# A conditioned transformer block: the first two norms with tokens on partitions, and five constant products ahead of them

## The chip, the cores and the metric

The kernel runs on one core of a Trainium2 chip. The metric is the device time of one execution in microseconds (us); lower is better. The median of three runs is given for a kernel. Five engines work side by side, each with its own queue of instructions: TensorE (PE in the profile; PEld is its loading of weights), VectorE (DVE), ScalarE (ACT), GpSimd (POOL) and SyncE (SP), which here issues most of the DMAs.

## The reference

One transformer block whose two norms are scaled and shifted by a condition `t` of each sequence. There are 4 sequences of 1024 tokens, 512 channels, 16 heads, a hidden width of 2048; everything is float32.

```python
def _tc_rmsnorm(x, t, gw, gb, bw, bb):
    g = (t @ gw.T + gb)[:, None, :]
    b = (t @ bw.T + bb)[:, None, :]
    inv_rms = jax.lax.rsqrt(jnp.mean(x * x, axis=-1, keepdims=True) + EPS)
    return g * x * inv_rms + b

def _L0_cond_ref(x, t, Wq, Wk, Wv, Wo, g1w, g1b, b1w, b1b, g2w, g2b, b2w, b2b, gate_w, hid_w, out_w):
    x = x + _attention(_tc_rmsnorm(x, t, g1w, g1b, b1w, b1b), Wq, Wk, Wv, Wo)
    return x + _swiglu(_tc_rmsnorm(x, t, g2w, g2b, b2w, b2b), gate_w, hid_w, out_w)

x = x + _L0_cond_ref(x, cond_256, ...)
```

The change touches only the first norm (g1, b1) of the first sequence, that is of its two halves of 512 tokens.

## The kernel before

Tokens come in eight blocks of 512, two to a sequence. A block lies in SBUF with channels on the 128 partitions: a tile `y[b, half]` of 128 x 4 x 512, where `C` = 4 groups of 128 channels stand side by side and the 512 tokens are columns. A norm therefore needs a sum over partitions for each token.

Up to line 740 lies the opening, with the tokens of the first sequence; after it the main loop runs over steps `g`. A step has the scores of one piece of attention on PE, the softmax of earlier ones on ACT and DVE, weighted values, and one or two chains of other work: first the projections that are left of the present and the next sequence (from `queue`), later the feed-forward network. At the end a short loop does what is left of the feed-forward network.

The order of the work on PE, DVE, ACT and POOL is the order in which the program issues it: each of these engines does its instructions one after the other, and one that waits holds up what is behind it. DMAs on SP are placed by a scheduler, so an early load can stand before the writes of the opening; each waits for its data and for a free buffer.

Buffers are named by a tag, with a number of buffers to each. The PSUM banks of tag `w` (pool `ps`, two of them) are shared by the sums of the norms (`pm`), the modulation (`pmod`) and two of three projections; the function `bank` gives every third projection the bank `wb` instead. In SBUF the squares of the opening and the staging of projected keys, queries and values take turns in tag `h` (seven buffers), the inverse of the first norm sits in tag `rmax`, that of the second in `tot`.

What the opening does, in the order of the program, is this:

- Loads on SP: the first half's tokens in four pieces (`load_y(0, 0)`), the modulation's weights for the first norm (`load_modw(0)`), weights of the first keys and queries (`load_wkq(0)`), the second half's tokens, the value weights `wv`, the modulation's second part, and two more weights of keys and queries.
- `norm_sum(y[0, 0], "a0_0")`, lines 210 to 220: for each channel group a square on ACT (line 215), and a product of the square with `ones_mean`, a 128 x 128 tile of 1/512 (line 216), all four summed in one PSUM bank. As the weights are all alike, each of the 128 partitions gets the mean of the squares for all 512 tokens. ACT takes the root (line 218), DVE the reciprocal (line 219), both of 128 x 512.
- `modulation(0)`: eight products of 128 x 128 weights with the condition, four columns each (line 722), and an addition on DVE (line 723).
- `norm_rest(0, 0, y[0, 0], "a0_0")`: for each channel group a multiplication by the inverse on DVE (`norm_scale`, line 199) and the modulation's scale and shift on ACT (`norm_mod`, line 202).
- Two projections of the first half, keys and queries (`project_kq`), eight products of 512 columns in all; every product goes through the helper `mm` (line 112).
- `norm_sum` for the second half, then the copies of the two projections out of PSUM on ACT with their DMA writes (the `evict` functions, lines 261 and 262).
- `norm_rest` for the second half.
- Four projections of values for the first half (`project_v`, lines 278 and 279 for copy and write); `modulation(1)`, for the second norm of the block, follows the first of them. Its weights share a buffer tag with the first residual load (line 435).
- One projection of keys for the second half. Then the main loop begins with the first scores (line 316).

The constant tiles that the change uses are there from the start: `ident`, the 128 x 128 identity, and `ones_mean`, which DVE fills at line 70.

Of the kernel before, what the change touches and what calls it, by code (L numbers as in the profile page):

```python
# [10 lines left out]
F32 = mybir.dt.float32  # L11
BF16 = mybir.dt.bfloat16
AF = mybir.ActivationFunctionType
ALU = mybir.AluOpType
# [3 lines left out]
P = 128  # L18
NB = 512
# [5 lines left out]
def tile_cond_transformer_block(  # L25
# [13 lines left out]
    nc = tc.nc  # L39
    NBLK, _, C, _ = x.shape  # L40
    B = cond_t.shape[1]
    D = C * P
# [3 lines left out]
    KT = L // P  # L46
# [11 lines left out]
    sb = ctx.enter_context(tc.tile_pool(name="sb", bufs=1))  # L58
    ps_sc = ctx.enter_context(tc.tile_pool(name="ps_sc", bufs=1, space=PSUM))
    ps_av = ctx.enter_context(tc.tile_pool(name="ps_av", bufs=1, space=PSUM))  # L60
    ps = ctx.enter_context(tc.tile_pool(name="ps", bufs=2, space=PSUM))
# [3 lines left out]
    ident = const.tile([P, P], F32, tag="ident", name="ident")  # L65
# [3 lines left out]
    ones_mean = const.tile([P, P], F32, tag="ones_mean", name="ones_mean")  # L69
# [3 lines left out]
    eps = const.tile([P, 1], F32, tag="eps", name="eps")  # L73
# [35 lines left out]
    def mm(dst, w, moving, start: bool, stop: bool, seeded: bool = False):  # L109
        n = columns[0]  # L110
        for k in range(0, P, n):
            nc.tensor.matmul(  # L112
                dst[k : k + n, :], w[:, k : k + n], moving, start=start, stop=stop, skip_group_check=seeded
            )

    y, wkq, wv, wo, kq, v = {}, {}, {}, {}, {}, {}
    raw, rmax, shift, mT, av, acc, avs, oT = {}, {}, {}, {}, {}, {}, {}, {}
    x2, res, h, fw, ow = {}, {}, {}, {}, {}
    bank_a, bank_b, fifth = {}, {}, {}
    state = {}  # L120
# [3 lines left out]
    def bank(name: str):  # L124

        if spare_bank[0]:
            spare_bank[0] = False
            return ps_av.tile([P, NB], F32, tag="av", name=name)
        turn[0] += 1
        if "sums" not in state and turn[0] % 3 == 0:  # L130
            return ps_b.tile([P, NB], F32, tag="wb", name=name)
        return ps.tile([P, NB], F32, tag="w", name=name)
# [65 lines left out]
    def norm_scale(dst, tag: str, c: int):  # L198
        nc.vector.tensor_tensor(dst[:, c, :], dst[:, c, :], state[tag], ALU.mult)

    def norm_mod(which: int, b: int, dst, c: int):
        nc.scalar.activation(  # L202
            dst[:, c, :],
            dst[:, c, :],
            AF.Identity,
            bias=mod[:, (2 * which + 1) * C + c, b : b + 1],
            scale=mod[:, 2 * which * C + c, b : b + 1],
        )

    def norm_sum(dst, tag: str):  # L210

        pm = ps.tile([P, NB], F32, tag="w", name=f"pm{tag}")
        for c in range(C):
            sq = sb.tile([P, NB], F32, tag="h", name=f"sq{tag}_{c}", bufs=7)
            nc.scalar.activation(sq, dst[:, c, :], AF.Square)
            nc.tensor.matmul(pm, ones_mean, sq, start=(c == 0), stop=(c == C - 1))
        inv = sb.tile([P, NB], F32, tag="rmax" if tag == "a0_0" else "tot", name=f"inv{tag}", bufs=1)
        nc.scalar.activation(inv, pm, AF.Sqrt, bias=eps)
        nc.vector.reciprocal(inv, inv)
        state[tag] = inv  # L220

    def norm_rest(which: int, b: int, dst, tag: str):
        for c in range(C):
            norm_scale(dst, tag, c)
            norm_mod(which, b, dst, c)
# [17 lines left out]
    def staging(name: str):  # L243

        if "sums" in state:
            return sb.tile([P, NB], F32, tag="ow", name=name, bufs=4)
        return sb.tile([P, NB], F32, tag="h", name=name, bufs=7)


    def project_kq(b: int, hg: int, which: int, half: int):  # L250
        pp = bank(f"pkq{b}_{hg}_{which}_{half}")
        for c in range(C):
            mm(pp, wkq[hg][:, which, c, :], y[b, half][:, c, :], c == 0, c == C - 1)

        def evict():
            scale = SCALE if which else 1.0
            if (b, hg) == (0, 0) and (which, half) != (1, 1):
                for i in range(NB // HQ):
                    k = half * NB // HQ + i
                    t = queries_tile(0, i) if which else keys_tile(0, k)  # L260
                    nc.scalar.activation(t, pp[:, i * HQ : (i + 1) * HQ], AF.Copy, scale=scale)
                    nc.sync.dma_start(out=kq_s[b, hg][:, which, k * HQ : (k + 1) * HQ], in_=t)
                return
            t = staging(f"st{b}_{hg}_{which}_{half}")
            nc.scalar.activation(t, pp, AF.Copy, scale=scale)
            nc.sync.dma_start(out=kq_s[b, hg][:, which, half * NB : (half + 1) * NB], in_=t)

        return evict

    def project_v(b: int, kt: int):  # L270
        half, col = divmod(kt * P, NB)
        pp = bank(f"pv{b}_{kt}")
        for c in range(C):
            mm(pp, y[b, half][:, c, col : col + P], wv[0][:, c, :], c == 0, c == C - 1)

        def evict():
            t = staging(f"sv{b}_{kt}")
            nc.scalar.copy(t, pp)
            nc.sync.dma_start(out=v_s[b][:, :, kt, :], in_=t.rearrange("p (a c) -> p a c", a=C))

        return evict
# [347 lines left out]
    for b in range(1, B):  # L629
        for half in range(QB):  # L630
            s = math.ceil((len(queue) + 1) / PACE)
            s4 = s - 4 - (s - 6) % UN
            tag = f"a{b}_{half}"
# [14 lines left out]
    for n in range(NBLK):  # L648
# [7 lines left out]
        if n < NBLK - 1:  # L656
            tag = f"f{n}"
# [30 lines left out]
    def fetch():  # L688

        if loads:  # L690
            load, a = loads.popleft()
            load(*a)
# [11 lines left out]
    with tc.manual_schedule(  # L704
# [8 lines left out]
        load_modw(1)  # L713
        fetch()
        fetch()
        norm_sum(y[0, 0], "a0_0")

        def modulation(k: int):
            pm = ps.tile([P, 4 * C, B], F32, tag="w", name=f"pmod{k}")
            cols = slice(k * 2 * C, (k + 1) * 2 * C)  # L720
            for i in range(k * 2 * C, (k + 1) * 2 * C):
                nc.tensor.matmul(pm[:, i, :], modw[:, i * P : (i + 1) * P], condT, start=True, stop=True)
            nc.vector.tensor_tensor(
                mod[:, cols, :], pm[:, cols, :], modb[:, cols].unsqueeze(2).to_broadcast([P, 2 * C, B]), ALU.add
            )

        modulation(0)
        norm_rest(0, 0, y[0, 0], "a0_0")
        evicts = [project_kq(0, 0, which, 0) for which in range(2)]
        norm_sum(y[0, 1], "a0_1")  # L730
        for evict in evicts:
            evict()
        norm_rest(0, 0, y[0, 1], "a0_1")
        for kt in range(KT // 2):
            project_v(0, kt)()
            if kt == 0:
                modulation(1)
        project_kq(0, 0, 0, 1)()

# [34 lines left out]
        while g < END:  # L774
# [10 lines left out]
            p = (g - FS) // 2  # L785
# [139 lines left out]
        for c, tag in enumerate(("rmax", "shift", "tot", "oT0")):  # L925
            sq = sb.tile([P, NB], F32, tag=tag, name=f"sqf{n}_{c}", bufs=1)
# [3 lines left out]
        for p in range(p0, NP_):  # L930
# [25 lines left out]
            if p == p0:  # L956
                pm = ps.tile([P, NB], F32, tag="w", name=f"pmf{n}")
                for c in range(C):
                    nc.tensor.matmul(pm, ones_mean, squares[c], start=(c == 0), stop=(c == C - 1))
                inv = sb.tile([P, NB], F32, tag="tot", name=f"invf{n}", bufs=1)  # L960
# [51 lines left out]
```

## Time and profile before

| what | value |
|---|---|
| runs before, median of 3 | 2450.79 us (2449.7 to 2451.94) |
| profiled execution, device time | 2455.29 us |
| profiled execution, span of its instructions | 2453.4 us |
| mean granted TensorE clock in it | 0.994 |
| PE busy | 2385.5 us (97%) |
| DVE busy | 1940.7 us (79%) |
| ACT busy | 1413.2 us (58%) |
| reciprocal of the opening's norms, DVE line 219 | 2 of 3353 ns |
| scaling in the opening, DVE line 199 | 8 of 686 ns |
| modulating in the opening, ACT line 202 | 8 of 801 ns |
| squares of the opening, ACT line 215 | 8 of 621 ns |

The span runs from the first to the last instruction; the device time has about 2 us around it. A line of a timeline has the start, the duration of the group, the engine, the line of the program, the operation, what it writes and reads, the shape and the count; in brackets stands the idle time of the engine before the group and what ended it. A line of a list of waits has the sum of the waits, their number and the longest. An instruction of PE that multiplies float32 appears as two passes, so that four products are x8. "PEclk" is the clock that TensorE was granted as a share of the full one; a stage's line gives for each engine its busy time within the stage.

### The profile page before, as it was taken

Reading aid. Unit: us, or ns where it says so; the run is one execution under the profiler, and the core shown is the slowest. Engines: PE = TensorE matmul, PEld = TensorE weight load, DVE = VectorE, ACT = ScalarE, POOL = GpSimd, SP = SyncE. Lnnn points to the kernel's source line nnn. Section 1 sums busy time; section 2 is a strip of 40 time slices with the busy share of each in tenths; the row PEclk is TensorE's granted clock in tenths of the full one; section 3 lists DMA queues with packets and bytes.
Section 4 is the critical chain, followed back from the end, with each engine's and each line's share of the span. In section 5 each row is a group of like instructions: output and inputs, shape, how many; then the busy total and the mean of one; then the engine's idle time right before and its main releaser. Section 6 shows DMA issues by size and latency. Waiting matters only on the chain. (4 is left out here: it accounts for less than half of the span.)

```text
span 2453.4 us, 72677 instructions
## 1 busy us (share of the span) xinstructions
PE 2385.5 (97%) x32553; PEld 1135.9 (46%) x32553; DVE 1940.7 (79%) x2183; ACT 1413.2 (58%) x1495; POOL 172.4 (7%) x207
## 2 busy tenths in 40 slices
PE   8999999999999999999999999999999999999999
PEld 3333334344444544544454544454445445444444
DVE  2688888878799988998899979997999799843332
ACT  3677776765566656665566656665666566512110
POOL 0000000000000000000000000000000000000000
PEclk9999999999999999999999999999999999999999
DMA  6599999988788788889888888898788888853442
GB/s 216 166 304 259 256 258 240 231 202 219 198 205 210 188 226 209 208 207 229 204 200 213 225 197 209 204 230 207 198 207 203 224 200 204 198 165 117 140 131 70
DMA packets 185988, 501.79 MB, mean 205 GB/s; under 512 B 21319, under 2 KB 78663, under 8 KB 158286
## 3 DMA queue, kind: packets, MB, share of 16 engines
q0 software_dynamic: 28656, 208.68, 43.9%
q1 hardware_dynamic: 156734, 288.47, 35.4%
q8 instruction: 256, 4.19, 0.7%
q14 instruction: 54, 0.44, 0.1%
q10 hardware_dynamic: 288, 0.01, 0.0%
HBM read 246.44 MB, written 41.97 MB: 118 GB/s over the span
## 5 line engine op out<-in xcount | busy, mean ns | idle before, releaser
L369 DVE TENSOR_TENSOR raw<-raw,shift 128x2048 f32<-128x2048 f32 (+1 forms) x320 | 588.8, 1857 | 25.6 <-ACT shift L364 25.6
L323 ACT COPY raw<-sc 128x2048 f32<-128x2048 f32 x256 | 479.7, 1874 | 187.4 <-PE sc L316 130.8
L372 ACT ACTIVATE raw<-raw 128x2048 f32<-128x2048 f32 x256 | 490.8, 1917 | 157.1 <-DVE raw L369 154.8
L328 DVE TENSOR_TENSOR rmax<-rmax,raw 128x1024 f32<-128x1024 f32 x384 | 469.5, 1223 | 48.8 <-ACT raw L323 42.2
L112 PE MATMUL pc<-h,ow 128*32 128x512 f32 x4096 | 470.5, 596 | 5.2 <-DMA ow<-in_out_w 4.2
L382 PE MATMUL av<-raw,v 128*32 128x256 f32 x4096 | 271.9, 383 | 35.6 <-ACT raw L372 35.1
L396 POOL DMA_DIRECT2D raw<-raw x192 | 165.3, 861 | 1967.4 <-ACT raw L372 878.9
L316 PE MATMUL sc<-q,k 32*128 32x256 f32 x4096 | 293.3, 400 | 1.0 <-ACT raw L323 1.0
L112 PE MATMUL pa<-x,fa 128*32 128x256 f32 x4096 | 272.5, 384 | 4.1 <-DVE pa L530 4.1
L112 PE MATMUL pa<-sums,fw 128*32 128x256 f32 x4096 | 271.5, 383 | 0.0
L112 PEld LDWEIGHTS pc<-h,ow 128*32 128x32 f32 x4096 | 128.6, 110 | 250.7 <-issue 231.9
L316 PEld LDWEIGHTS sc<-q,k 32*128 32x128 f32 x4096 | 184.9, 184 | 117.4 <-issue 75.8
L112 PE MATMUL pkq<-y,wkq 128*32 128x512 f32 (+1 forms) x1664 | 232.5, 594 | 4.3 <-ACT y L202 4.1
L112 PEld LDWEIGHTS pa<-x,fa 128*32 128x32 f32 x4096 | 124.7, 110 | 119.7 <-DVE pa L530 21.4
L382 PEld LDWEIGHTS av<-raw,v 128*32 128x32 f32 x4096 | 110.4, 109 | 149.4 <-ACT raw L372 66.0
L112 PEld LDWEIGHTS pa<-sums,fw 128*32 128x32 f32 x4096 | 134.4, 111 | 90.0 <-issue 3.4
L583 DVE SCALAR_TENSOR_TENSOR res<-pc,res 128x512 f32<-128x512 f32 x128 | 88.2, 689 | 78.9 <-PE pc L112 76.2
L545 ACT COPY pb<-pa 128x256 f32<-128x256 f32 x128 | 46.1, 360 | 174.4 <-PE pa L112 173.3
L562 ACT ACTIVATE t<-pa 128x512 f32<-128x512 f32 x128 | 78.1, 610 | 109.9 <-PE pa L112 109.6
L112 PE MATMUL pb<-x,fw 128*32 128x256 f32 x2048 | 134.0, 379 | 1.2 <-ACT pb L545 1.2
L112 PE MATMUL pa<-x,fw 128*32 128x256 f32 x2048 | 134.0, 379 | 0.0
L552 DVE TENSOR_TENSOR pb<-pb,p 128x256 f32<-128x256 f32 x128 | 55.0, 430 | 99.8 <-PE pb L112 94.2
(108 smaller groups left out, 2243.7 us busy)
## 6 DMA issues: line engine op xcount, KB each, us to landing
raw<-raw POOLq DMA_DIRECT2D x192, 1024.0 KB, 9.3
fw<-sw SPq DMA_DIRECT2D x128, 512.0 KB, 7.8
fa<-in_gh_w SPq DMA_DIRECT2D x128, 384.0 KB, 6.8
ow<-in_out_w SPq DMA_DIRECT2D x128, 256.0 KB, 3.1
wkq<-in_kq_w SPq DMA_DIRECT2D x32, 512.0 KB, 6.2
v<-vs SPq DMA_DIRECT2D x128, 128.0 KB, 6.6
k<-kqs SPq DMA_DIRECT2D x124, 128.0 KB, 6.5
kqs<-st SPq DMA_DIRECT2D x61, 256.0 KB, 8.3
```

The lines of the kernel that those rows point to most:

```text
L112: nc.tensor.matmul(dst[k : k + n, :], w[:, k : k + n], moving, start=start, stop=stop, skip_group_check=seeded)
L316: nc.tensor.matmul(sc[:, i, k, :], keys[rows, k * P : (k + 1) * P], queries[rows, :], start=True, stop=True)
L323: nc.scalar.copy(raw[r].rearrange("p k h q -> p h k q"), state.pop(("sc", r)))
L328: nc.vector.tensor_tensor(rmax[j], rmax[j], raw[r][:, k, :, :], ALU.max)
L369: nc.vector.tensor_tensor(t, t, s.unsqueeze(1).to_broadcast(list(t.shape)), ALU.add)
L372: nc.scalar.activation(raw[r], raw[r], AF.Exp)
L382: nc.tensor.matmul(av[j][i * DH : (i + 1) * DH, :], v[m, u][:, k, i * DH : (i + 1) * DH], raw[r][:, k, i, :], start=(kt == 0), stop=(kt == ...
L396: nc.gpsimd.dma_start(out=acc[j].rearrange("p k h q -> p (k h q)"), in_=raw[r].rearrange("p k h q -> p (k h q)"), accum_op=ALU.add,)
L545: nc.scalar.copy(bank_b[p][:, RIGHT], bank_a[p][:, RIGHT])
L552: nc.vector.tensor_tensor(b[:, LEFT], b[:, RIGHT], fifth.pop(p), ALU.subtract)
L562: nc.scalar.activation(state["t", p], bank_a[p], AF.Tanh, scale=0.5)
L583: nc.vector.scalar_tensor_tensor(r, pp, 0.5, r, ALU.mult, ALU.add)
```

## The change

`norm_sum` is rewritten. The four squares are now added up on DVE (three additions of 128 x 512). Four products then take 128 tokens each as weights and one column of `ones_mean` as the moving operand, so that the mean of token `p` of group `t` lands on partition `p` in column `t` of a 128 x 4 PSUM tile. Root (ACT) and reciprocal (DVE) are of 128 x 4. One DVE instruction multiplies the identity by these columns and by 512 into `diagonal`, four 128 x 128 diagonal matrices side by side. `norm_sum` returns a function `spread_root`, which multiplies `ones_mean` with the diagonals (512 columns): each partition gets the inverse of all 512 tokens, in PSUM, where `norm_scale` now reads it.

The caller issues `spread_root` of the first half after `modulation(0)`. For the second half the first projection of values, with its copy and its write, is moved ahead of `spread_root` and `norm_rest`; `modulation(1)` now follows the second projection of values. Ahead of the first `norm_sum` stand five products of `ones_mean` with itself, repeated to 512 columns, into a PSUM tile that nothing reads.

```diff
     def norm_sum(dst, tag: str):
 
-        pm = ps.tile([P, NB], F32, tag="w", name=f"pm{tag}")
+
+        sq = [sb.tile([P, NB], F32, tag="h", name=f"sq{tag}_{c}", bufs=7) for c in range(C)]
         for c in range(C):
-            sq = sb.tile([P, NB], F32, tag="h", name=f"sq{tag}_{c}", bufs=7)
-            nc.scalar.activation(sq, dst[:, c, :], AF.Square)
-            nc.tensor.matmul(pm, ones_mean, sq, start=(c == 0), stop=(c == C - 1))
-        inv = sb.tile([P, NB], F32, tag="rmax" if tag == "a0_0" else "tot", name=f"inv{tag}", bufs=1)
-        nc.scalar.activation(inv, pm, AF.Sqrt, bias=eps)
-        nc.vector.reciprocal(inv, inv)
-        state[tag] = inv
+            nc.scalar.activation(sq[c], dst[:, c, :], AF.Square)
+            if c:
+                nc.vector.tensor_tensor(sq[0], sq[0], sq[c], ALU.add)
+        nt = NB // P
+        pm = ps.tile([P, nt], F32, tag="w", name=f"pm{tag}")
+        for t in range(nt):
+            nc.tensor.matmul(pm[:, t : t + 1], sq[0][:, t * P : (t + 1) * P], ones_mean[:, 0:1], start=True, stop=True)
+        few = sb.tile([P, nt], F32, tag="few", name=f"few{tag}", bufs=2)
+        nc.scalar.activation(few, pm, AF.Sqrt, bias=eps)
+        nc.vector.reciprocal(few, few)
+        diagonal = sb.tile([P, nt, P], F32, tag="t", name=f"diagonal{tag}", bufs=2)
+        nc.vector.scalar_tensor_tensor(
+            diagonal,
+            ident.unsqueeze(1).to_broadcast([P, nt, P]),
+            float(D),
+            few.unsqueeze(2).to_broadcast([P, nt, P]),
+            ALU.mult,
+            ALU.mult,
+        )
+
+        def spread_root():
+            inv = ps.tile([P, NB], F32, tag="w", name=f"inv{tag}")
+            nc.tensor.matmul(inv, ones_mean, diagonal.rearrange("p t q -> p (t q)"), start=True, stop=True)
+            state[tag] = inv
+
+        return spread_root
...
-        norm_sum(y[0, 0], "a0_0")
+
+        ahead = ps.tile([P, NB // P, P], F32, tag="w", name="ahead")
+        for _ in range(5):
+            nc.tensor.matmul(
+                ahead, ones_mean, ones_mean.unsqueeze(1).to_broadcast(list(ahead.shape)), start=True, stop=True
+            )
+        spread_root = norm_sum(y[0, 0], "a0_0")
...
         modulation(0)
+        spread_root()
         norm_rest(0, 0, y[0, 0], "a0_0")
         evicts = [project_kq(0, 0, which, 0) for which in range(2)]
-        norm_sum(y[0, 1], "a0_1")
+        spread_root = norm_sum(y[0, 1], "a0_1")
         for evict in evicts:
             evict()
+        project_v(0, 0)()
+        spread_root()
         norm_rest(0, 0, y[0, 1], "a0_1")
-        for kt in range(KT // 2):
+        for kt in range(1, KT // 2):
             project_v(0, kt)()
-            if kt == 0:
+            if kt == 1:
                 modulation(1)
         project_kq(0, 0, 0, 1)()
```

## The prediction

> **What bounds the kernel now.** The page comes first: TensorE (PE) is busy 97% of the span, VectorE (DVE) 79%, ScalarE (ACT) 58%. The list of waits says how little PE waits on anything: 35.1 us for the exponentials in 37 pieces, and a few single ones, among them these.
>
> ```profile
> PE pma L216 <- ACT sqa L215: 5.5, 1, 5.5
> PE pc L112 <- DMA ow<-in_out_w: 4.2, 1, 4.2
> PE pkq L112 <- ACT y L202: 4.1, 1, 4.1
> POOL raw L396 <- DMA raw<-raw: 502.7, 54, 13.7
> ```
>
> So PE sets the end, and what brings its work forward in the opening brings the end forward, unless a later wait takes it back. I therefore read the opening in the timeline, first PE (start, duration, in brackets the idle time before):
>
> ```profile
> 5.49 5.17 PE L216 MATMUL pma<-sqa,ones_mean 128*128 128x512 f32 x8 [5.49 <-ACT sqa L215]
> 10.51 1.84 PE L722 MATMUL pmod<-condT,modw 128*128 128x4 f32 x16
> 16.41 9.97 PE L112 MATMUL pkq<-y,wkq 128*128 128x512 f32 x16 [4.05 <-ACT y L202]
> 26.21 3.60 PE L216 MATMUL pma<-sqa,ones_mean 128*128 128x512 f32 x8
> 30.59 3.70 PE L112 MATMUL pv<-wv,y 128*128 128x512 f32 x8 [0.78 <-ACT inva L218]
> 34.12 1.84 PE L722 MATMUL pmod<-condT,modw 128*128 128x4 f32 x16
> 36.61 10.57 PE L112 MATMUL pv<-wv,y 128*128 128x512 f32 x24 [0.64 <-DVE mod L723]
> 47.01 3.60 PE L112 MATMUL pkq<-y,wkq 128*128 128x512 f32 x8
> 50.54 1.15 PE L316 MATMUL sc<-q,k 32*128 32x256 f32 x16
> ```
>
> Every f32 product is two passes: the x8 at 47.01 are four products, 0.43 us a pass. The x16 at 16.41 take 9.80 us until the next start where 16 x 0.43 is 6.88. The stages by granted clock (span of the stage, PE busy, PEld, DVE, ACT, POOL, then PEclk) say why:
>
> ```profile
> 5.03:8.44 3.41, 2.95 (x4) 1.40 (x5) 0.00 (x0) 3.06 (x5) 0.00 (x0) 1.00 1.04 372
> 11.86:15.27 3.41, 0.49 (x5) 0.40 (x4) 3.41 (x3) 0.00 (x0) 0.00 (x0) 1.00 1.02 424
> 15.27:18.69 3.42, 2.29 (x3) 1.17 (x4) 2.04 (x4) 3.15 (x5) 0.00 (x0) 0.51 1.05 424
> 18.69:22.10 3.41, 3.41 (x5) 1.35 (x4) 0.00 (x0) 1.85 (x4) 0.00 (x0) 0.50 0.99 395
> 790.10:793.51 3.41, 1.64 (x32) 0.59 (x26) 3.41 (x6) 3.27 (x3) 0.51 (x1) 1.00 0.94 244
> 2169.08:2172.49 3.41, 1.66 (x28) 0.56 (x20) 1.23 (x1) 0.41 (x2) 0.00 (x0) 1.00 0.90 339
> ```
>
> The clock changes on a grid of 3.41 us. After the stage from 11.86, busy 0.49, it is halved; a stage with 2.29 busy does not restore it, one with 3.41 does, as 2.95 did at 8.44 (the recorded 1.00 before 8.44 is only the lack of a record: passes there took 0.85). Four stages in the body with 1.64 busy were each followed by a half clock; the one with 1.66 was not. So the limit for staying fast lies near 48% busy. The other engines (ACT's and DVE's timelines):
>
> ```profile
> 10.71 0.69 ACT L218 ACTIVATE inva<-pma,eps 128x512 f32<-128x512 f32 x1 [1.74 <-PE pma L216]
> 11.43 3.35 DVE L219 RECIPROCAL inva<-inva 128x512 f32<-128x512 f32 x1 [9.06 <-ACT inva L218]
> 14.81 2.50 DVE L199 TENSOR_TENSOR y<-y,inva 128x512 f32<-128x512 f32 x4
> ```
>
> The 3.35 us reciprocal of a whole 128x512 tile stands between the sums and the first scaling.
>
> **First norm.** The last square ends at 7.67. New: a DVE add of 0.69 (the 128x512 add of L141) to 8.41, the two earlier ones hidden under the squares; then eight narrow passes. No row has one column moving; the nearest, the modulation, does 16 passes in 1.84, so 0.92, and at most 8 x 0.25 (their full duration) = 2.0. I take 0.92: from 8.47, with 0.19 for the first weights, to 9.58, visible at 9.7. Root 0.30 and reciprocal 0.17 (the 128x4 rows of L173 and L177), diagonal 0.69 (scalar_tensor_tensor of L583; at most 1.23, the 128x1024 row of L328, for its broadcast operands): ready at 11.0. Meanwhile PE does the modulation, 1.84, to 11.42, its weights having landed at 8.4 (2.60 + 5.8). The spreading product, 0.43 + 0.59, ends at 12.44, so DVE scales from 12.49 where it was 14.81. Reading that operand from PSUM costs nothing visible: L583 reads PSUM and takes 689 ns against 684. **Gain 2.32.** With the narrow passes at 2.0, about 1.1 of it is lost. The key and query weights must be there at 14.09 (12.49 plus the present 1.60 from first scaling to first projection): they were issued at 3.08, ahead of the second half's tokens, whose transfers issued near 6 landed 6.5 later, so by 12.6.
>
> **The five products ahead** start near 1.1, when the memset of the ones is done (0.84 + 0.17), and wait for no DMA. Ten passes: at 0.85 until a full grid stage has gone by (5.0 in this execution's grid), then 0.43: done at 7.4; over all positions of the grid 6.9 to 8.8, so under the squares and the add that end at 8.4. Without that cover they would cost what they end later than 8.47. What they buy is a fast clock at 14.09. It holds if the gap from 12.44 to 14.09, 1.65 us, leaves every stage at least 1.76 busy: above 1.66, by 0.1. Then sixteen passes take 6.88, not 9.80: **gain 2.92** against this execution. It stood badly on the grid, though. Cold stretches last from about 2.6 us (a stage must be nearly full) to 6.0, mean 4.3, and cost half of that; this one ran 5.7. In the mean I take **2.2**; bounds 0 and 3.0.
>
> [...]
>
> **Second norm**, from the end of the projections to the first scores: 50.54 - 26.21 = 24.33 now. New: narrow passes 0.92 (for 3.60); the wait for the bank 0.39 (0.78 less the root's 0.69 - 0.30); the value projection now moved ahead 3.53; spreading product 0.86; three more projections 10.40; modulation 1.85; keys 3.53: 21.48. The wait of 0.64 for the modulation's add goes, since the projection after it takes another bank. **Gain 2.85.** The second diagonal is ready about 1.3 us after the sums, under the 3.53 of the moved projection; without that cover its reciprocal, add and diagonal would stand on PE, some 1.2. Behind it DVE scales 2.5 us while PE does the next projection (3.47), so the modulation's bank is free in time. The moved projection also issues an ACT copy (0.58), which now goes ahead of the four modulating activations, and one 256 KB write on SP; these writes are read back for products at 94.42. The modulation moves one projection back; SP's residual load, which waited for it at 36.00, still comes earlier, by about 4. POOL has nothing here.
>
> **Sum.** 2.32 + 2.92 + 2.85 = 8.1 on the profiled execution: 2455.29 (span 2453.4 and 1.9 around it) becomes 2447.2. The runs shown lie 4.5 lower, at 2450.79; with the mean clock term, 7.4 off: **2443.4**.
>
> **Rivals.** (1) The narrow passes do not count as busy: then from 7.4 to 14.09 only the 1.02 of the spreading product does, some stage falls under 1.65 whatever the grid, and the clock is halved again. Mean cold stretch as before, so no clock gain; spreading product +0.43, modulation about +0.5: 1.4 + 2.85 = 4.3, **2446.5**. For: 0.49 of such passes did not save the stage from 11.86. Against: no stage shows them alone. (2) The constants do not warm the clock, so the change does not do what it says: ten slow passes end at 9.7, narrow ones at double time (0.23) plus the modulation reach about 15.2, the first projection 18.9, 2.5 late; the second norm's 2.85 is left: **2450.5**. Against: the same ones with squares did warm it by 8.44. (3) Slower: the first output-weight load, PE's 4.2 us wait at 592 with a half clock after it, shares the DMA with 1 MB accumulations. Seven us earlier, it can fall behind one more; POOL's longest wait for one is 13.7. From 7.4 more waiting it decides; at 13.7, **2457.1**. For: DMA is over 80% busy there. Against: loads and products shift together.
>
> **Chances.** Forecast 0.56; rival 1 0.28; rival 2 0.07; rival 3 0.09. The runs of this kernel tell about 0.2% (4.9 us, the line at 2445.9) from no change. Faster: 0.54 of the forecast and 0.13 of rival 1 (its grid positions spread over +-1.7), 0.67. Same: 0.02 + 0.14 + 0.06 + 0.02 = 0.24. Slower: 0.07 of rival 3 and 0.01 each of rivals 1 and 2: 0.09. Range: low end the full 8.1 and one half-clocked stage of the body (1.7) less, 2441; high end rival 1 plus one such stage, 2448.5, which also covers the narrow passes at 2.0.
>
> **What would show it.** First scaling near 12.5, first projection near 14.1 with passes of 0.43 and no half clock before 50 us; first scores near 42.5; first projected value 0.4 after the narrow sums. Passes of 0.85 at 14.1 mean rival 1; slow narrow passes, rival 2; a wait over 11 us at the first output weights, rival 3. A first projection later than 15.5 with a fast clock would make the first step wrong.

## The result, and the profile after

The changed kernel takes 2443.22 us (median of 22 runs, 2440.21 to 2451.12), the kernel before 2450.14 us in as many runs beside them (2444.69 to 2455.69). The ratio of the two is 0.9975, with a 95% interval of 0.9968 to 0.9982. The forecast was 2443.4, worked out from three runs of the kernel before with a median of 2450.79.

The profiled execution of the changed kernel is the longest of its 22: 2451.12 us, with a span of 2449.3 against 2453.4. So its end says little, and its opening is read instead. First PE's timeline of the changed kernel (start, duration, what ended the idle time):

```profile
1.06 7.60 PE L739 MATMUL ahead<-ones_mean 128*128 128x512 f32 x10 [1.06 <-DVE eps L74]
8.74 1.05 PE L221 MATMUL pma<-ones_mean,sqa 128*128 128x1 f32 x8
9.66 1.93 PE L748 MATMUL pmod<-condT,modw 128*128 128x4 f32 x16
11.45 1.10 PE L237 MATMUL inva<-diagonala,ones_mean 128*128 128x512 f32 x2
14.18 8.74 PE L112 MATMUL pkq<-y,wkq 128*128 128x512 f32 x16 [1.63 <-ACT y L202]
22.76 0.95 PE L221 MATMUL pma<-ones_mean,sqa 128*128 128x1 f32 x8
24.06 3.70 PE L112 MATMUL pv<-wv,y 128*128 128x512 f32 x8 [0.35 <-ACT fewa L223]
27.60 1.02 PE L237 MATMUL inva<-diagonala,ones_mean 128*128 128x512 f32 x2
...
44.21 1.15 PE L336 MATMUL sc<-q,k 32*128 32x256 f32 x16
```

The first projections start at 14.18, where it was 16.41; their sixteen passes take 8.58 us until the next start, where it was 9.80; from there to the first scores it is 21.45, where it was 24.33. The first scores come 6.33 us earlier. DVE's timeline of the same kernel shows the first norm's small pieces and the scaling that follows them:

```profile
10.13 0.18 DVE L224 RECIPROCAL fewa<-fewa 128x4 f32<-128x4 f32 x1 [1.38 <-ACT fewa L223]
10.22 0.38 DVE L87 CAST select<-pick 12x512 bf16<-12x512 f32 x1
10.54 0.67 DVE L226 SCALAR_TENSOR_TENSOR diagonala<-ident,fewa 128x512 f32<-128x512 f32 x1
11.62 0.19 DVE L749 TENSOR_TENSOR mod<-pmod,modb 128x32 f32<-128x32 f32 x1 [0.41 <-PE pmod L748]
12.59 2.48 DVE L199 TENSOR_TENSOR y<-y,inva 128x512 f32<-128x512 f32 x4 [0.77 <-PE inva L237]
```

The small pieces cost what the prediction took from the nearest rows. A cast left over from the setup (0.38) slips in between, without harm: the diagonal is there at 11.21, and PE comes from the modulation to the spreading product only at 11.45. The scaling starts 2.22 us earlier than before.

But sixteen passes in 8.58 us are not 0.43 each. The stages of the changed kernel by granted clock (span, then PE, PEld, DVE, ACT and POOL busy, then PEclk, DMA share and GB/s) show a half clock exactly where the prediction had none:

```profile
7.21:10.62 3.41, 3.32 (x21) 2.25 (x19) 1.93 (x6) 2.16 (x3) 0.00 (x0) 1.00 1.00 349
10.63:14.04 3.41, 1.92 (x11) 1.09 (x10) 2.22 (x5) 0.73 (x2) 0.00 (x0) 1.00 1.05 430
14.04:17.45 3.41, 3.27 (x4) 1.51 (x5) 1.17 (x3) 3.41 (x7) 0.00 (x0) 0.50 1.01 412
```

PE was busy for 1.92 us of the middle stage and the clock fell to 0.50 after it; in the body of the kernel before, the stage from 2169.08, with 1.66, had kept it. What differs is what PE was busy with: 0.8 us of that stage are narrow passes of the modulation (four columns), only 1.1 the spreading product. The experiments ask whether that is the cause.

### The profile page after: what moved, and what is told of

The parts are those of the page before. It is cut to its first block, busy times and chain, and to the rows that moved or that the text cites. A ratio compares the mean times of both kernels' runs of the same rounds, so it can differ in the third digit from the quotient of the medians.

```text
span 2449.3 us, 72718 instructions
## 1 busy us (share of the span) xinstructions
PE 2389.4 (98%) x32567; PEld 1137.2 (46%) x32567; DVE 1940.2 (79%) x2191; ACT 1412.1 (58%) x1495; POOL 172.4 (7%) x207
## 5 line engine op out<-in xcount | busy, mean ns | idle before, releaser
L112 PE MATMUL pb<-sums,fa 128*32 128x256 f32 x2048 | 133.9, 379 | 0.0
```

Of the source, the lines that this page charges most:

```text
L112: nc.tensor.matmul(dst[k : k + n, :], w[:, k : k + n], moving, start=start, stop=stop, skip_group_check=seeded)
```

## The experiments

Theory A: a pass that streams few columns counts for little in whatever grants the clock, so the five products' fast clock is lost again before the first projections. Theory B: narrow passes count like others, and the half clock has another cause (the 1.63 us gap ahead of the projections) or is rare. Where PE stood in the profiled execution of each kernel (starts and durations in us; the passes are counted until the next start on PE):

| kernel | first projection | its 16 passes | first scores |
|---|---|---|---|
| before | 16.41 | 9.80 | 50.54 |
| changed | 14.18 | 8.58 | 44.21 |
| changed, second and third execution | 14.45, 13.94 | 8.98, 8.36 | 44.88, 43.75 |
| narrow products ahead | 17.56 | 9.12 | 48.14 |
| no products ahead | 16.91 | 9.46 | 47.82 |
| kernel before with products ahead | 17.60 | 10.04 | 51.97 |
| widened, two executions | 13.90, 13.86 | 6.97, 6.97 | 42.43, 42.39 |
| widened, gap filled, two executions | 13.80, 13.99 | 6.97, 6.97 | 42.32, 42.51 |
| gap filled only | 15.09 | 7.10 | 43.64 |
| first norm only | 14.00 | 8.58 | 48.61 |
| no move of the values | 14.75 | 8.59 | 46.10 |

### Narrow products alone ahead

```diff
-        for _ in range(5):
-            nc.tensor.matmul(
-                ahead, ones_mean, ones_mean.unsqueeze(1).to_broadcast(list(ahead.shape)), start=True, stop=True
-            )
+        for _ in range(18):
+            nc.tensor.matmul(ahead[:, 0, 0:4], ones_mean, ones_mean[:, 0:4], start=True, stop=True)
```

> The changed kernel with eighteen products of four columns (36 narrow passes) in place of the five of 512 columns. PE is then occupied from about 1.1 us on by narrow passes alone. Theory A (narrow passes do not count as busy): no full clock is granted before the first projections at 14 us are well under way; the narrow passes themselves, at a slow clock throughout, step by more than the 0.115 us of the modulation, about 0.2, and end near 8.7; passes of the first projections start at 0.85. Theory B (they count): the record shows a rise to the full clock between 4.5 and 8 us.

PE's timeline of this kernel, and three of its stages:

```profile
1.06 7.84 PE L739 MATMUL ahead<-ones_mean 128*128 128x4 f32 x36 [1.06 <-DVE eps L74]
8.76 1.85 PE L221 MATMUL pma<-ones_mean,sqa 128*128 128x1 f32 x8
10.47 3.55 PE L746 MATMUL pmod<-condT,modw 128*128 128x4 f32 x16
13.88 2.06 PE L237 MATMUL inva<-diagonala,ones_mean 128*128 128x512 f32 x2
17.56 9.29 PE L112 MATMUL pkq<-y,wkq 128*128 128x512 f32 x16 [1.62 <-ACT y L202]
```

```profile
4.86:8.27 3.41, 3.41 (x17) 3.41 (x18) 2.01 (x4) 2.53 (x4) 0.00 (x0) 1.00 1.01 362
18.52:21.93 3.41, 3.41 (x5) 1.35 (x4) 1.13 (x2) 3.18 (x6) 0.00 (x0) 1.00 0.56 234
21.94:25.35 3.41, 3.41 (x9) 1.52 (x8) 0.93 (x2) 0.00 (x0) 0.00 (x0) 1.00 0.00 0
```

The stage from 4.86 is filled by PE and by its weight loads, and the clock does not rise, although the record says 1.00 in it and in the others. The passes themselves tell: five 512-column passes in the full stage up to 21.93, nine in the next, so the rise came at 21.93; 0.213 us each in the modulation, (13.88 - 10.47) / 16, against 0.112 in the changed kernel, and 2.06 for the spreading product against 1.10. From 1.06 to 13.88 PE showed no idle time and stayed slow. So four-column passes did not raise the clock here, as theory A has it; whether they fail to keep it is the next question. There is one run of this kernel, 2449.93 us, too few to compare times.

### The narrow products widened

The four products of the sums and the eight of the modulation stream 128 columns; each overwrites what the one before left beyond its own columns.

```diff
-            nc.tensor.matmul(pm[:, t : t + 1], sq[0][:, t * P : (t + 1) * P], ones_mean[:, 0:1], start=True, stop=True)
+            nc.tensor.matmul(pm[:, t : t + P], sq[0][:, t * P : (t + 1) * P], ones_mean, start=True, stop=True)
...
-                nc.tensor.matmul(pm[:, i, :], modw[:, i * P : (i + 1) * P], condT, start=True, stop=True)
+                nc.tensor.matmul(
+                    wide[:, i * B : i * B + P].rearrange("p (r b) -> p r b", b=B),
+                    modw[:, i * P : (i + 1) * P],
+                    condT.unsqueeze(1).to_broadcast([P, P // B, B]),
+                    start=True,
+                    stop=True,
+                )
```

> The changed kernel with the narrow products widened: the four products of the sums and the eight of the modulation stream 128 columns each (the columns that are not needed are overwritten by the next product or not read), so that a pass is occupied by its columns for about 0.107 of its 0.115 us. Theory A (narrow passes do not count, which is why the clock fell at 14 us in the profiled execution of the changed kernel): no half clock between 8 and 40 us, sixteen passes of the first projections in 6.9 us, first scores at 42.5 to 42.8 us, and 1.3 to 3.0 us less than the changed kernel in the time. Theory B (it fell for another reason, such as the 1.63 us gap before the first projections): a half clock at 14 us again in about as many executions, and the same time as the changed kernel.

The 0.107 us there is an estimate, a quarter of the 0.43 us that a pass of 512 columns took in the kernel before.

PE's timeline of the widened kernel, and its stage before the projections:

```profile
9.46 1.95 PE L749 MATMUL pmod<-condT,modw 128*128 128x128 f32 x16
11.25 1.02 PE L237 MATMUL inva<-diagonala,ones_mean 128*128 128x512 f32 x2
13.90 7.13 PE L112 MATMUL pkq<-y,wkq 128*128 128x512 f32 x16 [1.63 <-ACT y L202]
20.87 1.05 PE L221 MATMUL pma<-ones_mean,sqa 128*128 128x128 f32 x8
```

```profile
10.66:14.08 3.42, 1.79 (x10) 0.96 (x10) 2.16 (x5) 1.05 (x2) 0.00 (x0) 1.00 1.07 437
14.08:17.49 3.41, 3.41 (x9) 1.49 (x10) 1.17 (x3) 3.41 (x7) 0.00 (x0) 1.00 0.99 402
```

The grid lies as in the changed kernel's profile (a stage ends at 14.08, there at 14.04), the gap of 1.63 us is the same, PE is even a little less busy (1.79 against 1.92), and the clock stays (1.00; the sixteen passes take 6.97 us). The wider passes cost nothing (1.95 us for sixteen against 1.93). The first scores come 1.78 us earlier than in the changed kernel. The median is 2442.84 us (9 runs), with a ratio to before of 0.9965 (0.9953 to 0.9977). These runs do not show the expected 1.3 to 3.0 us below the changed kernel; the runs of all kernels are put together further down.

### Without the five products, and the five products alone

The first takes the five products out of the changed kernel, the second puts them into the kernel before, ahead of its `norm_sum`.

> The changed kernel without the five products ahead. Theory A (the fast clock that they bring is lost again before the first projections): the sums and the modulation run at the slow clock, which puts the first projections 1 to 2.5 us later; their own slow stretch is as long on average as with the five products; time 1 to 2.5 us above the changed kernel. Theory B (in most executions the clock lasts until the projections): 2.2 us more on top of that, 3 to 5 us above the changed kernel.

> The kernel before with the five products ahead, nothing else. Both theories: the sums of the first norm run at the full clock, but they wait for the last square at 7.7 anyway and end about 1 to 1.5 us earlier at most (four products, 8 passes at 0.43, the last two after the last square); then 4 us of nothing on PE, so the clock is halved before the first projections as before. Time 0 to 2 us below the kernel before. If the five products were worth their 2.2 us by themselves, the first projections would run at 0.43 a pass from the start.

PE's timeline without the five products:

```profile
8.08 1.87 PE L221 MATMUL pma<-ones_mean,sqa 128*128 128x1 f32 x8 [8.08 <-DVE pick L82]
9.81 3.55 PE L743 MATMUL pmod<-condT,modw 128*128 128x4 f32 x16
13.22 2.05 PE L237 MATMUL inva<-diagonala,ones_mean 128*128 128x512 f32 x2
16.91 9.63 PE L112 MATMUL pkq<-y,wkq 128*128 128x512 f32 x16 [1.63 <-ACT y L202]
```

The median is 2447.22 us (11 runs), ratio to before 0.9989 (0.9980 to 0.9999); against all runs of the changed kernel the mean is 4.2 us higher (95% interval 2.2 to 6.4, by resampling the runs). Theory A's size was too small, and B's reason was not the one: the first projections start 2.73 us later (16.91 against 14.18), because sums, modulation and spreading product take 1.73, 3.41 and 2.05 us one after the other (0.92, 1.79 and 1.10 in the changed kernel), and the sixteen passes of the projections lose another 0.9 (9.46 against 8.58). So the five products earn most of their worth between 8.7 and 12.5 us, on the narrow passes and the spreading product, and less in the projections that they were meant for.

In the kernel before they are in the way. Its timeline with them:

```profile
1.06 7.37 PE L718 MATMUL ahead<-ones_mean 128*128 128x512 f32 x10 [1.06 <-DVE eps L74]
8.26 3.60 PE L216 MATMUL pma<-sqa,ones_mean 128*128 128x512 f32 x8
11.70 1.84 PE L727 MATMUL pmod<-condT,modw 128*128 128x4 f32 x16
17.60 10.21 PE L112 MATMUL pkq<-y,wkq 128*128 128x512 f32 x16 [4.05 <-ACT y L202]
```

The expectation missed this: there the sums' products ran under the squares from 5.49 on, and now all eight passes stand behind the constants, so the first projection starts 1.19 us later. The first scores are 1.43 later than before in the profile; the median of 11 runs is 2448.88 us, with a ratio of 0.9992 (0.9983 to 1.0001). No difference is shown in the time.

### The gap filled, with wide and with narrow products

After `spread_root()` of the first half:

```diff
         modulation(0)
         spread_root()
+        bridge = ps.tile([P, 7, 64], F32, tag="w", name="bridge")
+        for _ in range(2):
+            nc.tensor.matmul(
+                bridge, ones_mean, ones_mean[:, :64].unsqueeze(1).to_broadcast(list(bridge.shape)), start=True, stop=True
+            )
```

> The widened kernel (narrow products made 128 columns wide) with two more products of constants, 448 columns each, between the spreading product and the first projections, 1.5 us of the 1.63 us gap there. Theory A (the clock is lost by too little counted work in a stage of 3.41 us, narrow passes and the gap together): no position of the grid is left in which the clock can fall, so no half clock in the opening in any execution, first projections at 13.9 us with 0.43 a pass, scores near 42.4, and the time at or up to 1 us below the widened kernel. Theory B (the constants in the gap stand in the projections' way): first projections 0.3 us or more later than 13.9 and the time above the widened kernel.

> The changed kernel with the two products of constants in the gap, but narrow products as they are. Theory A (narrow passes count for little): stages that lie between 8.7 and 12.1 still hold too little, so the clock falls before the first projections in most positions of the grid; it comes back sooner, as PE is busy throughout from 11.2 on, at most 3.41 us after the fall, so the slow stretch within the first projections is 0 to 2 us long and their sixteen passes take 6.9 to 8 us. Theory B (the gap is the cause): no half clock in the opening, sixteen passes in 6.9 us.

With wide products the clock stays (sixteen passes in 6.97 us) and the first projections start at 13.80 (13.99 in a second execution), less than 0.3 later than the 13.90 without the filling, so the constants are not in the way. With narrow products, PE's timeline and stages read:

```profile
10.96 1.10 PE L237 MATMUL inva<-diagonala,ones_mean 128*128 128x512 f32 x2
11.90 3.08 PE L757 MATMUL bridge<-ones_mean 128*128 128x448 f32 x4
15.09 7.26 PE L112 MATMUL pkq<-y,wkq 128*128 128x512 f32 x16
```

```profile
8.59:12.00 3.41, 3.41 (x26) 2.93 (x26) 1.27 (x4) 0.45 (x2) 0.00 (x0) 1.00 0.95 294
12.00:15.42 3.42, 3.31 (x6) 1.17 (x5) 2.48 (x4) 2.60 (x4) 0.00 (x0) 0.50 1.02 426
```

The stage from 8.59 has no idle time on PE at all, and the clock is 0.50 after it. Theory B is out: no gap is left in this stage, and the clock is lost all the same. As expected by A the slow stretch is over soon (passes of the projections 7.10 in all), but the filling itself, 3.08 us where it takes 1.67 with wide products, holds the first projections up until 15.09. The medians are 2442.51 us (7 runs, ratio 0.9974, 0.9963 to 0.9985) for wide and filled, 2441.87 (12 runs, 0.9970, 0.9959 to 0.9982) for filled only; the latter's mean is not told from the changed kernel's (1.4 lower, from 3.7 lower to 1.0 higher).

### The two halves of the change, and the cover of the second

> The changed kernel with the second half's norm as it was before (sums over 512 columns, reciprocal of the whole tile, values after it). By the steps of the prediction the stretch from the end of the first projections to the first scores is 24.3 us again instead of 21.45, so first scores 2.9 us later than the changed kernel, and the time 2.9 us above it. Rival: DVE's 3.35 us reciprocal was hidden there anyway, and the stretch shrinks by less than 1 us.

> The changed kernel without the move: all four projections of values follow the second spreading product, the modulation's second part the first of them. The root, the reciprocal and the diagonal, some 1.6 us from the end of the narrow sums, then stand on PE where 0.35 us of waiting stands now: first scores 1.2 us later than the changed kernel relative to the end of the first projections (21.45 becomes 22.7). Rival: the move mattered for the banks as well, the wait of 0.64 us behind the modulation's addition comes back too, and it is 1.9 us.

With the second half's norm as it was, the stretch from the end of the first projections to the first scores is 26.03 us (48.61 - 22.58); it holds another half clock, from 34.35 on, that costs 1.7 (the 24 passes from 32.98 take 12.26 us, 10.57 in the kernel before), and without that it is 24.3: the old length. The stage before that fall is another witness: of its 2.77 us of busy PE 1.40 are narrow passes of the modulation, and 1.37 are wide.

```profile
30.94:34.35 3.41, 2.77 (x16) 1.99 (x16) 1.99 (x5) 3.30 (x5) 0.00 (x0) 1.00 0.63 234
34.35:37.77 3.42, 3.42 (x5) 1.33 (x4) 0.00 (x0) 0.11 (x1) 0.00 (x0) 0.50 0.98 355
```

Median 2449.07 us (11 runs, ratio 0.9988, 0.9979 to 0.9997); mean 4.0 above all runs of the changed kernel (2.0 to 5.8), which holds the expected 2.9; the nine runs of the changed kernel taken beside these are too few to tell (2.4 above them, from 0.7 below to 5.3 above). The rival, that DVE's reciprocal was hidden, is out by the profile: the stretch shrinks by 2.9, not by less than 1.

Without the move of the first projection of values, the edit is its two lines of order:

```diff
-        project_v(0, 0)()
         spread_root()
         norm_rest(0, 0, y[0, 1], "a0_1")
-        for kt in range(1, KT // 2):
+        for kt in range(KT // 2):
             project_v(0, kt)()
-            if kt == 1:
+            if kt == 0:
```

PE's timeline then:

```profile
23.34 0.95 PE L221 MATMUL pma<-ones_mean,sqa 128*128 128x1 f32 x8
25.67 1.10 PE L237 MATMUL inva<-diagonala,ones_mean 128*128 128x512 f32 x2 [1.39 <-DVE diagonala L226]
26.61 3.60 PE L112 MATMUL pv<-wv,y 128*128 128x512 f32 x8
30.04 1.84 PE L748 MATMUL pmod<-condT,modw 128*128 128x4 f32 x16
32.17 10.57 PE L112 MATMUL pv<-wv,y 128*128 128x512 f32 x24 [0.28 <-DVE mod L749]
```

1.39 us of waiting for the diagonal where 0.35 was, and 0.28 of the modulation's wait come back: 46.10 - 23.34 = 22.76, expected 22.7. The time does not settle it. The median is 2448.1 us (11 runs, ratio 0.9989, 0.9979 to 0.9999); the mean is 3.9 above all runs of the changed kernel (1.6 to 5.9), further off than 1.3 us, but 2.3 above the nine taken beside these (from 0.9 below to 5.4 above), which holds 1.3. Whether the move is worth more than the profile shows stays open.

### The changed kernel and the widened ones again

> The changed kernel once more, beside the others. Theory A (narrow passes count for little): in most positions of the grid the clock falls before or at the start of the first projections; another execution shows a half clock there again, of other length. Theory B: the half clock at 14 us in the first profile was a rare one, and this execution shows none. Median within 2 us of 2443.2.

> The changed kernel a third time, beside the widened ones. Theory A: a half clock before or at the start of the first projections again, their sixteen passes 8.4 to 9.8 us. Theory B: none. Median 2442 to 2446.

> The widened kernel a second time, for another position of the grid. Only the 1.63 us gap before the first projections is left in it, which leaves 1.78 us of a stage busy, 0.1 above what the body of the kernel before needed to keep its clock. Theory A: no half clock in the opening again, sixteen passes of the first projections in 7.0 us, first scores at 42.4 to 42.8. If the limit lies higher than 1.78 for these products, a half clock begins between 13.8 and 15.5 in some executions.

> The widened kernel with the gap filled, a second time. Theory A: no half clock in the opening, first scores at 42.3 to 42.6, and, with the runs of the job before, a median 1 to 3 us below the changed kernel.

The changed kernel's opening was profiled five times in all (three executions of it, and the two kernels of the section before, which share its first norm). The clock fell in each: at 14.04, 11.70 and 13.35 in the three executions; in the other two the passes tell, with sixteen in 8.58 us from 14.00 for the first norm only, and 1.99 us for the spreading product from 11.14 and sixteen in 8.59 without the move. With the gap filled only it fell at 12.00. None of the four executions with wide products shows a fall in the opening (spreading product 1.02 us, sixteen passes 6.97 in each). The two of them without the filling had nearly the same position of the grid, that of the changed kernel's first profile (stages end at 14.08 and 14.03), so other positions are seen only with the filling. Of the changed kernel the third execution has the fastest projections, 8.36 us, just under the 8.4 expected; the second has the slowest, 8.98 us, with these stages, two of them at the half clock:

```profile
8.29:11.70 3.41, 3.17 (x25) 2.92 (x26) 1.27 (x4) 0.46 (x2) 0.00 (x0) 1.00 0.97 315
11.70:15.11 3.41, 1.78 (x3) 0.50 (x2) 2.25 (x4) 1.53 (x3) 0.00 (x0) 0.50 1.03 428
15.11:18.53 3.42, 3.42 (x5) 1.35 (x4) 1.07 (x3) 3.42 (x6) 0.00 (x0) 0.50 1.04 418
```

The medians: changed 2445.53 us (9 runs, ratio 0.9985, 0.9972 to 0.9997), 2.3 from 2443.2 where at most 2 was expected, and in the next set of runs 2443.65 (12 runs, 0.9974, 0.9964 to 0.9984); in that set widened 2441.21 (8 runs, 0.9964, 0.9951 to 0.9978), widened and filled 2438.56 (6 runs, 0.9955, 0.9941 to 0.9970). With all runs put together, the means are: before 2450.5 (100 runs), changed 2444.3 (43), widened 2442.5 (17), widened and filled 2441.6 (13). Against the changed kernel the widened one is 1.8 lower (interval from 3.7 lower to 0.2 higher), the widened and filled one 2.7 (0.6 to 4.8). So widened and filled is the one version that is shown to be faster than the changed kernel as well as the one before. Widening alone brings the first scores earlier in the profile, but a shorter time is not shown for it; that filling adds anything to widening is not shown, neither by the time nor by the profile (first scores 42.32 and 42.51 against 42.43 and 42.39).

## Why the prediction was right, and which step of it was not

**The bound.** That PE sets the end, and that time gained in the opening stays gained, held. From the first scores to 134 us of the kernel before, the changed kernel's lead over it does not move by 0.01 us, and where it moves later, it moves mostly with half clocks of the one or the other and with the wait for the first output weights. The opening gives 6.3 us in the profile, and the mean of 43 runs against 100 is 6.2 lower (5.1 to 7.3).

**First norm**, 2.32 predicted: the first scaling stands at 12.59 (12.49 predicted), the first projection at 14.18 (14.09), a gain of 2.23. The eight narrow passes took 0.92, as taken from the modulation's row, the reciprocal 0.18, the diagonal 0.67. The nearest rows gave the prices. The 0.92 holds at the full clock only: without the five products the same passes took 1.73 (8.08 to 9.81).

**Second norm**, 2.85 predicted: 2.88. The parts fit one by one: wait for the bank 0.35 (0.39), spreading product 0.89 (0.86), no wait at the modulation. The moved projection hides about what was said, 1.3 against 1.2, by the profile of the kernel without the move. One side remark was off: the residual load comes 2.1 us earlier (33.90 against 36.00), not 4.

**The five products ahead** is the step that failed: "What they buy is a fast clock at 14.09." They were done at 8.66, as foreseen (6.9 to 8.8), and the clock rose at 7.21, but it was gone before the first projections in five executions of five. The prediction let every busy microsecond of PE count: it asked for 1.76 in each stage, the stage up to 14.04 had 1.92, and the clock fell. It fell as rival 1 had it, and the sign, passes of 0.85 at 14.1, was there: with 0.8 us of narrow passes among the 1.92 the clock was not kept.

Rival 1's price was too high, though. It added 0.9 for a slow modulation and a slow spreading product, and took the slow stretch in the projections to be as long as before. In fact the narrow passes of the first norm ran before the fall, and the sixteen passes took 8.6 us on average (8.58, 8.98, 8.36, 8.58, 8.59), where the four openings that enter the projections slow needed 9.6 (9.80, 9.46, 10.04, 9.12). The clock term, taken as 2.2 from an estimate of the slow stretches (2.6 to 6.0 us, as a stage with 2.29 us busy had not brought the clock back and one with 2.95 had), thus measures about 1.0 to 1.2, on few executions. With 2.2 for the first norm and 2.9 for the second that is 6.1 to 6.3, not 7.4, and the mean of all runs is 6.2 lower.

That the median fell within 0.2 us of the forecast is partly luck. The forecast started from 2450.79, and the kernel before measured 2450.14 beside the changed one; the two later sets of runs put the changed kernel 5.8 and 6.1 below the kernel before. The mean of its 43 runs, 2444.3, lies 0.9 above the forecast and 2.2 below rival 1's 2446.5, so the time alone would not have told that the clock fell as in rival 1. The widened kernel shows the sum as it was meant: 8.11 us at the first scores, for 8.1 predicted against the profiled execution.

Whether narrow passes count as busy was open before the runs, and the prediction gave 0.28 to the case that they do not. No run shows that as a rule. What one shows is that a busy PE was not enough: with the gap filled only, PE was busy for all 3.41 us of the stage from 8.59, some 2.4 of them with narrow passes, and the clock was 0.50 after it.

**The other signs.** "No half clock before 50 us" and "first scores near 42.5" failed with this step (44.21). Rival 2 is out: with the five products of constants the clock rose near 7.2 (weight loads of 0.34 us up to 6.34, 0.20 at 7.19), without them only within the first projections, at about 22 by an estimate from their length (9.46 us from 16.91, that is six passes at 0.85 and ten at 0.43). Rival 3 did not come: PE's wait for the first output weights is 2.3 us, 4.2 before.

## What to carry to other kernels

When products are put ahead to raise TensorE's clock, look at what runs between them and the work that is to profit: a PE kept busy for 3.41 us, some 2.4 of them with narrow passes, did not hold the clock here. Where narrow products stand there, let them stream 128 columns if a pass takes no longer for it; sixteen took 1.95 us here, 1.93 with four columns, and the clock stayed in the opening (four executions), though the gain in time by itself, 1.8 us, is not clear of the noise. And read the worth of an opening from the opening: with half clocks scattered over the body, single executions of one kernel lie 10 us apart (2440.21 to 2451.12 for the changed one).

## What the runs showed of the hardware

- A stage of 3.41 us in which PE was busy throughout with four-column passes did not raise the clock (narrow products ahead, from 4.86; passes of 0.213 us after it). One in which PE was busy throughout with narrow passes and some 1.0 us of wide ones did not keep it (gap filled only, from 8.59; 0.50 after it). Whether narrow passes count for something stays open: the stage from 7.21 of the changed kernel had about 1.45 us of wide and 1.9 us of narrow passes, and the clock held until the next stage; the one from 30.94 of the kernel with the first norm only had 1.37 and 1.40, and it did not.
- A pass that loads weights of 128 columns and streams 1 or 4 took 0.112 to 0.115 us with the five products ahead (changed kernel) and 0.213 to 0.216 without them; with 128 streamed columns a pass of the modulation took 0.112 as well (widened).
- The half clocks go a long way to explain the scatter between executions. One such stage cost PE 1.7 us (12.26 against 10.57 for the same 24 passes). After the opening the profiled execution of the kernel before had six (from 595.5, 793.5, 1052.9, 1827.8 and 2087.2 us, the first half clock two stages long), the changed kernel's first, the longest of its 22 runs, seven (from 133.5, 590.9, 1560.3, 1819.7, 2079.1 and 2164.4, the last one two stages long). Over these 22 runs the mean granted clock was 0.994 in the two longest (2451.12 and 2449.71 us) and 0.998 in the two shortest (2440.21 and 2440.24).
